# Part of a gate product moved into the recurrences of a four-layer stack, one addition moved to GpSimd, and new order lists

## The chip, the cores and the metric

The kernel runs on one core of a Trainium2 chip. Its time is in microseconds (us) of the device for one execution. TensorE is called PE (PEld is its loading of weights), VectorE DVE, ScalarE ACT, GpSimd POOL, and SP is the engine that issues all of this kernel's DMAs.

## The reference

The input x has 32 rows (batch) of 256 time steps with 256 features. Four layers are added to it one after the other; each has a condition of 256 features per row.

```python
x = x + L0(cond, x)   # GRU over time: z, r gates, hh = tanh(xh + r*h @ U + vh)
x = x + L1(cond, x)   # h = tanh(h * (1 - alpha) + sigmoid(h @ Wh.T + x_t @ Wz.T + b) * x_t)
x = x + L2(x, cond)   # gated cumulative sum
x = x + L3(x, cond)   # low-rank adapted MLP with gelu

# L2
f = sigmoid(x @ W_f.T + b_f);  i = sigmoid(x @ W_i.T + b_i)
gate_sum = f + i + EPS
candidate = x @ W_h.T + b_h
new_info = i / gate_sum * candidate
log_cumprod = cumsum(log(f / gate_sum + EPS), axis=1)
scaling = exp(log_cumprod[:, -1:] - padded[:, :-1])
hidden = cumsum(scaling * new_info) + exp(log_cumprod) * initial_hidden
```

L0 and L1 are recurrences: each of 256 steps needs the step before. The products of L2 (f, i and the candidate c) need only the finished x of their own time steps.

## The kernel before

**Two stages.** The first runs the two recurrences, step by step, layer 1 one step behind layer 0 (lines 726 to 804). The second runs the last layers, L2 and L3, over eight groups of four rows. The program fixes the order on every engine: each engine carries out its instructions in the order in which the code issues them.

**A step of the recurrences** issues on PE, in this order: U_rz (products of hT for the gates r and z), what falls due in the table `products`, w_1z (layer 1's product with its input, named w_l_Wz in the profile), U_h after r*h has been formed and transposed (rhT), w_1h, then W_rzh, the input products of the next step. `product` (line 601) cuts each into small products by quadrants of the array. Every fourth step a new bank of layer 0 is begun (line 633), every eighth one of layer 1 (at t % 8 == 2). On DVE a step has rh, rhT, keep (line 764), pieces of other work, the scan that forms h (line 672), hT, a transposition and the scan for layer 1. On POOL it has the residual of line 722 and the pairs of line 787.

**Tables of extra work.** `at(when, t, f, ...)` puts a piece of other work at step t in one of the tables products, sigmoids, sums, additions, moves, transfers; `due` issues it there. So the matrices of layer 3 are made (32 steps have such a product, line 507), and so are gates of L2: time is cut into NH = 8 stretches of CT = 32 steps, and once a stretch is finished, the gates f and i of its steps are computed for blocks of CB = 8 rows and halves e of the features. A unit (h, q, e) of `gate_unit` (line 103) has two tiles, f and i, each of two products over k; each product is 128x256. A free step takes one product; near the end five steps take two, which are then cut by quadrants. Then come the two sigmoids, the sum s = f + i (`add_up`), g = f + EPS*s (`guard`), and three stores into DRAM (`waiting`). This is done for the first NW_H = 6 of the 8 stretches.

**The last layers.** `STAGES` (line 967) names the pieces of work on a group: in (fetch the stored gates), lf, ls, lg (gates of the two late stretches, their sum and guard), c (`candidate`, the product with W_c over all eight stretches for two rows, 128x512), m (`weigh`, (c + b) * i on DVE), ln (logarithms on ACT), sum (the scan cc for the cumulative sum, DVE), w (`exponents`, one addition on DVE), exp (ACT), new and cum (DVE: times i, then a scan), h0 (DVE), x (`add_hidden`, an addition of 128x512 on POOL), mid, last and y (the two products and the end of layer 3). `HEAD` is the order of the first pieces, and `TURN` is the order for one turn; it is repeated for turns 2 to 9, where pieces of groups that do not exist are left out. A word such as `sum:1.0` is row 1, half 0 of the group. A turn works on several groups at once: stage 0 (lf to ln) on one group, sum and exp on the group before it, the rest on that or the one before.

`add_hidden` makes its POOL addition wait for the last DVE instruction that was issued ahead of it in the list (`on_vector`). On ACT, functions from another table need a table load (lines 846, 951, 1009).

Of the kernel before, what the change touches and what calls it, by code (L numbers as in the profile page):

```python
# [10 lines left out]
AF = mybir.ActivationFunctionType  # L11
ALU = mybir.AluOpType
# [4 lines left out]
B = 32  # L17
T = 256
# [11 lines left out]
CB = 8  # L30
NH = T // CT
NW_H = 6
EPS = 1e-8


# [4 lines left out]
def kernel(ctx: ExitStack, tc: tile.TileContext, a, out: bass.AP):  # L40
# [26 lines left out]
    def vec(name, c):  # L67
        i = VECS.index(name)
        return vecs[:, i, c : c + 1]
# [21 lines left out]
    def gate_product(ps, w, e, k, rows, h0, h1):  # L91

        nc.tensor.matmul(  # L93
            ps[:, 0 : (h1 - h0) * (rows.stop - rows.start) * CT].rearrange(
                "p (h b t) -> p h b t", h=h1 - h0, t=CT
            ),
            w[:, k, e * P : (e + 1) * P],
            X2[:, k, rows, h0 * CT : h1 * CT].rearrange("p b (h t) -> p h b t", t=CT),
            start=(k == 0),
            stop=(k == NC - 1),  # L100
        )

    def gate_unit(h, q, e, banks):

        t = {}

        def multiply(name, w, k, by_quadrants):
            rows = slice(q * CB, (q + 1) * CB)
            if not by_quadrants:
                gate_product(banks[name], w, e, k, rows, h, h + 1)  # L110
                return

            for j in range(Q):
                js = slice(j * SQ, (j + 1) * SQ)
                nc.tensor.matmul(
                    banks[name][js].rearrange("p (b t) -> p b t", t=CT),
                    w[:, k, e * P + js.start : e * P + js.stop],
                    X2[:, k, rows, h * CT : (h + 1) * CT],
                    start=(k == 0),
                    stop=(k == NC - 1),  # L120
                    skip_group_check=True,
                    tile_position=(0, j * SQ),
                )

        def unit_tile(name):
            t[name] = gu.tile([P, CB * CT], FP, name=f"gate_{name}", tag=f"gate_{name}")
            return t[name]

        def sigmoid(name):
            nc.scalar.activation(  # L130
                unit_tile(name), banks[name], AF.Sigmoid, bias=vec("b_" + name, e)
            )

        def add_up():
            nc.vector.tensor_add(unit_tile("s"), t["f"], t["i"])

        def guard():
            nc.vector.scalar_tensor_tensor(  # L138
                unit_tile("g"), t["s"], EPS, t["f"], ALU.mult, ALU.add
            )  # L140

        def store(name):
            nc.sync.dma_start(out=waiting[q][:, "gsi".index(name), e, h], in_=t[name])

        return multiply, sigmoid, add_up, guard, store

    parts_f = {}

# [19 lines left out]
    gi = ctx.enter_context(tc.tile_pool(name="gates_in", bufs=1))  # L168
    gated = {}

    def fetch_chunk(g, i, e, hs=slice(0, NW_H)):
        name = "gsi"[i]
        if e == hs.start == 0:
            pool, bufs = (gp, 2) if i == 2 and g % 3 else (gi, 1)
            gated[name, g] = pool.tile(
                [P, NC, NH, GB * CT], FP, name=f"in_{name}", tag=f"in_{name}", bufs=bufs
            )
        q, half = divmod(g, CB // GB)
        cols = slice(half * GB * CT, (half + 1) * GB * CT)
        nc.sync.dma_start(out=gated[name, g][:, e, hs], in_=waiting[q][:, i, e, hs, cols])  # L180

    def fetch(g, i):
        for e in range(NC):
# [16 lines left out]
    with ExitStack() as rec:  # L200
# [43 lines left out]
        def at(when, t, f, *args):  # L244
            when.setdefault(t, []).append((f, args))
# [307 lines left out]

        free = [t for t in range(CT + 3, T) if t not in products]
        twice = range(T - 14, T - 4, 2)
        free = sorted(free + list(twice))
        stored = {}
        for h in range(NW_H):  # L560
            for q in range(B // CB):
                for e in range(NC):
                    while free[0] < (h + 1) * CT + 3:
                        free.pop(0)
                    multiply, sigmoid, add_up, guard, store = gate_unit(
                        h, q, e, {"f": pg[:, 0], "i": pg[:, 1]}
                    )
                    for name, w in (("f", w_f), ("i", w_i)):
                        ts, free[:NC] = free[:NC], []
                        for k, t in enumerate(ts):  # L570
                            by_quadrants = any(t in twice for t in ts)
                            at(products, t, multiply, name, w, k, by_quadrants)
                        at(sigmoids, t, sigmoid, name)
                    at(sums, t + 1, add_up)
                    at(sums, t + 2, guard)
                    for n, name in enumerate("isg"):
                        stored[q] = t + 2 + n // 2 + (n == 2)
                        at(transfers, stored[q], store, name)
# [19 lines left out]
        def due(when, t):  # L598
            return [f(*args) for f, args in when.get(t, ())]
# [85 lines left out]
        def by_chunk(x):  # L685
            return x.rearrange("p (c b) -> p c b", b=B)
# [22 lines left out]
        with tc.manual_schedule():  # L709
# [16 lines left out]
            for t in range(T + 1):  # L726
# [15 lines left out]
                    finish_1()  # L742
                    late = None
                due(moves, t)
                due(products, t)
# [105 lines left out]
        )  # L851

    def late(g, name, e):
        return gated[name, g][:, e, LATE].rearrange("p h n -> p (h n)")

    def late_sum(g, e):
        return nc.vector.tensor_add(late(g, "s", e), parts_f[g, e], late(g, "i", e))
# [3 lines left out]
            late(g, "g", e), late(g, "s", e), EPS, parts_f.pop((g, e)), ALU.mult, ALU.add  # L861
        )

    def candidate(g, u):
        r, e = divmod(u, NC)
        b0 = g * GB + r * 2
        ps = pp.tile([P, 512], FP, name="ps_c", tag="ps_c")
        pcs[g, u] = ps.rearrange("p (h n) -> p h n", h=NH)
        for k in range(NC):
            gate_product(ps, w_n, e, k, slice(b0, b0 + 2), 0, NH)  # L870

    def weigh(g, u):
        r, e = divmod(u, NC)
        m = gated["i", g][:, e, :, r * 2 * CT : (r + 1) * 2 * CT]
        return nc.vector.scalar_tensor_tensor(
            m, pcs.pop((g, u)), vec("b_c", e), m, ALU.add, ALU.mult
        )

    def logs(g, q):
# [77 lines left out]
    def finish(g, b):  # L957
# [15 lines left out]
    }  # L973

    TURN = """
        lf:0 new:2 new:3 cum:2 sum:0.0 mid:1 in:2 mid:0 sum:1.0 cum:3 h0:2.0 lf:1 sum:0.1
        sum:3.1 last:1 sum:1.1 sum:3.0 w:1 exp:1 h0:3.1 h0:2.1 w:0 ls:0 h0:3.0 ls:1 c:0
        sum:2.0 w:3 lg:0 lg:1 x:2 m:0 y:1 x:3 exp:0 last:0 c:1 m:1 exp:3 c:3 y:0 mid:2 mid:3
        new:1 sum:2.1 new:0 w:2 cum:0 cum:1 c:2 h0:0.1 h0:0.0 exp:2 ln:1 h0:1.1 h0:1.0 ln:0
        last:2 x:1 m:3 last:3 y:2 in:1 x:0 m:2 in:0 y:3  # L980
    """

    HEAD = """
        in:2@2 lf:0@0 ls:0@0 lf:1@0 lg:0@0 c:2@0 c:1@0 ls:1@0 lg:1@0 ln:1@0 m:2@0 m:1@0
        sum:2.1@0 sum:2.0@0 c:0@0 ln:0@0 m:0@0 w:2@0 sum:3.1@0 sum:0.1@0 in:2@1 in:1@1
        sum:3.0@0 sum:0.0@0 sum:1.1@0 w:0@0 lf:0@1 lf:1@1 c:3@0 sum:1.0@0 ls:1@1 c:3@1 m:3@0
        exp:0@0 in:0@1 w:1@0 m:3@1 new:0@0 exp:1@0 lg:1@1 ls:0@1 new:1@0 w:3@0 exp:2@0
        cum:1@0 c:1@1 cum:0@0 h0:1.0@0 h0:0.0@0 exp:3@0 h0:1.1@0 lg:0@1 ln:1@1 x:1@0 ln:0@1
        c:2@1 m:1@1 c:0@1 h0:0.1@0 in:1@2 x:0@0 m:2@1 m:0@1 in:0@2
    """  # L990

    with tc.manual_schedule():
# [82 lines left out]
```

## Time and profile before

Three runs took 951.61 us at the median (950.96 to 952.18). The profiled execution has a span of 950.9 us.

| engine | busy, us | share of the span | instructions |
|---|---|---|---|
| PE | 919.3 | 97% | 22822 |
| DVE | 788.3 | 83% | 3409 |
| ACT | 573.3 | 60% | 2652 |
| POOL | 236.0 | 25% | 594 |

Some groups of the profile (line, engine, output from inputs, shape, count, busy us, mean ns of one):

| group | count | busy | mean |
|---|---|---|---|
| L93 PE ps_c from X, w_W_c, 128x512 | 128 | 61.5 | 613 |
| L93 PE pg from X, w_W_f, 128x256 | 176 | 61.5 | 431 |
| L938 PE ps_l from X, wt, 128x256 | 256 | 60.7 | 392 |
| L135 DVE gate_s from gate_f, gate_i, 128x256 | 48 | 22.2 | 462 |
| L875 DVE in_i from ps_c, vecs, in_i, 128x512 | 32 | 23.9 | 746 |
| L903 DVE w from cc, s, 128x512 | 32 | 21.7 | 678 |
| L960 DVE y from ps_l, X, 128x512 | 32 | 22.0 | 689 |
| L931 POOL X from X, w, 128x512 | 32 | 41.0 | 1291 |
| L722 POOL X from pairs, h1T, 128x64 | 256 | 102.7 | 401 |
| L467 POOL wn from wn, b, 128x128 | 16 | 7.2 | 450 |

How to read it: a product in fp32 shows as two records on PE. Busy time of a group counts overlapping instructions once; PE's ends are modelled, so for PE the distance from start to start tells more than the length. The recurrences run from 14 to about 736 us of the span, the last layers from there to the end.

### The profile page before, as it was taken

To read this page: it belongs to the slowest core of one execution; us is meant where nothing else is said; L and a number is where in the kernel's file an instruction comes from. 1 tells how busy PE (TensorE), PEld (TensorE's weight loads), DVE (VectorE), ACT (ScalarE), POOL (GpSimd) and SP (SyncE) were. 2 spreads that over 40 slices of the span, in tenths; PEclk is the share of its full clock that TensorE was granted. 3 is DMA by queue.
4 is the path that set the end of the run, shared out by engine and by line. 5 is a ranking of instruction groups with operands and counts; after the bars stand their busy time and mean duration, and the time that the engine had idled before them with its cause. 6 is when DMAs were issued, how large, how long until landed. Compare 5 with 4: busy or idle time off the path is not lost.

```text
span 950.9 us, 55227 instructions
## 1 busy us (share of the span) xinstructions
PE 919.3 (97%) x22822; PEld 630.0 (66%) x22822; DVE 788.3 (83%) x3409; ACT 573.3 (60%) x2652; POOL 236.0 (25%) x594
## 2 busy tenths in 40 slices
PE   7999999999999999999999999999999799999978
PEld 4666666666666666666666666666676467777756
DVE  5777788888888888888888888888877899999995
ACT  3455555555555555555555555555555878889973
POOL 1233322222222222222222222222222012222222
PEclk9999999999999999999999999999999999999989
DMA  8345212222222222222222222341232457777643
GB/s 259 114 118 156 80 52 87 71 73 91 70 88 78 86 76 66 92 71 87 72 72 92 66 92 66 121 131 61 83 115 74 132 166 231 230 219 223 190 156 124
DMA packets 109726, 107.72 MB, mean 113 GB/s; under 512 B 9857, under 2 KB 96673, under 8 KB 109474
## 3 DMA queue, kind: packets, MB, share of 16 engines
q1 hardware_dynamic: 109474, 104.19, 35.2%
q8 instruction: 179, 2.93, 1.4%
q14 instruction: 73, 0.60, 0.2%
HBM read 59.06 MB, written 45.09 MB: 110 GB/s over the span
## 4 chain that ended last, share of the span: by engine, by line
PE 81%; DVE 11%; ACT 3%; issue 2%; DMA 1%; SPq 0%; POOL 0%; DVEq 0%; POOLq 0%; ACTq 0%
PE p L606 46%; PE ps_l L938 11%; PE pg L93 10%; PE ps_c L93 5%; DVE h L672 5%; PE p L633 3%; PE ps_g L93 2%; PE pw L510 2%; ACT other L690 2%; DVE hT L682 1%; ACT r L690 1%; DVE cc L897 1%; DMA w_W_rzh<-in_W_rzh_dram 1%; DVE rh L760 1%; DVE gate_g L138 1%
## 5 line engine op out<-in xcount | busy, mean ns | idle before, releaser
L606 PE MATMUL p<-w_W_rzh,xT 128*32 128x192 f32 x4096 | 213.8, 326 | 0.7 <-DMA w_W_rzh<-in_W_rzh_dram 0.7
L690 ACT ACTIVATE other<-p 128x32 f32<-128x32 f32 x512 | 74.3, 200 | 171.6 <-PE p L606 171.6
L672 DVE TENSOR_TENSOR_SCAN h<-other,keep 128x64 f32<-128x64 f32 x512 | 121.3, 279 | 66.3 <-ACT other L690 62.9
L606 PE MATMUL p<-w_U_rz,hT 128*32 128x128 f32 x4080 | 166.1, 279 | 6.4 <-issue 0.3
L787 POOL TENSOR_TENSOR pairs<-xT,hT 128x64 f32<-128x64 f32 x256 | 82.3, 322 | 327.1 <-DVE other L803 301.9
L690 ACT ACTIVATE r<-p 128x32 f32<-128x32 f32 x510 | 72.8, 195 | 149.9 <-PE p L606 149.9
L722 POOL TENSOR_TENSOR X<-pairs,h1T 128x64 f32<-128x64 f32 x256 | 102.7, 401 | 214.7 <-DVE rhT L682 211.1
L606 PEld LDWEIGHTS p<-w_U_rz,hT 128*32 128x32 f32 x4080 | 97.0, 108 | 85.8 <-DVE hT L682 83.7
L672 DVE TENSOR_TENSOR_SCAN pre<-other,pairs 128x128 f32<-128x128 f32 x256 | 123.4, 482 | 33.9 <-ACT pairs L794 0.2
L606 PEld LDWEIGHTS p<-w_W_rzh,xT 128*32 128x32 f32 x4096 | 124.4, 110 | 22.9 <-DMA w_W_rzh<-in_W_rzh_dram 1.4
L606 PEld LDWEIGHTS p<-w_l_Wz,pairs 128*32 128x32 f32 x4096 | 78.2, 110 | 84.7 <-issue 69.3
L794 ACT ACTIVATE pairs<-h1T,leak 128x32 f32<-128x32 f32 x510 | 133.6, 314 | 0.4
L606 PE MATMUL p<-w_l_Wz,pairs 128*32 128x64 f32 x4096 | 119.2, 225 | 3.5 <-ACT keep L740 0.9
L606 PE MATMUL p<-w_U_h,rhT 128*32 128x64 f32 x4080 | 106.2, 221 | 0.0
L606 PE MATMUL p<-w_l_Wh,h1T 128*32 128x64 f32 x4080 | 104.1, 219 | 0.0
L760 DVE TENSOR_TENSOR rh<-r,h 128x32 f32<-128x32 f32 x510 | 75.0, 189 | 32.2 <-ACT r L690 6.2
L682 DVE STREAM_TRANSPOSE hT<-h 128x32 f32<-128x32 f32 x512 | 84.2, 198 | 0.0
L931 POOL TENSOR_TENSOR X<-X,w 128x512 f32<-128x512 f32 x32 | 41.0, 1291 | 162.3 <-DVE in_g L860 99.5
L682 DVE STREAM_TRANSPOSE rhT<-rh 128x32 f32<-128x32 f32 x510 | 80.0, 195 | 0.0
L606 PEld LDWEIGHTS p<-w_l_Wh,h1T 128*32 128x32 f32 x4080 | 76.2, 110 | 0.1
L606 PEld LDWEIGHTS p<-w_U_h,rhT 128*32 128x32 f32 x4080 | 69.6, 108 | 5.0
L719 ACT ACTIVATE h1T<-pre 128x64 f32<-128x64 f32 x256 | 69.7, 272 | 1.1 <-DVE pre L672 1.1
(110 smaller groups left out, 1472.7 us busy)
## 6 DMA issues: line engine op xcount, KB each, us to landing
adapted<-wm SPq DMA_DIRECT2D x128, 128.0 KB
wt<-adapted SPq DMA_DIRECT2D x28, 512.0 KB
w<-in_W_dram SPq DMA_DIRECT2D x32, 256.0 KB
out_dram<-y SPq DMA_DIRECT2D x32, 256.0 KB
xT<-in_xT_dram SPq DMA_DIRECT2D x60, 128.0 KB
gates<-gate_i SPq DMA_DIRECT2D x48, 128.0 KB
gates<-gate_s SPq DMA_DIRECT2D x48, 128.0 KB
gates<-gate_g SPq DMA_DIRECT2D x48, 128.0 KB
```

Of the source, the lines that this page charges most:

```text
L93: nc.tensor.matmul(ps[:, 0 : (h1 - h0) * (rows.stop - rows.start) * CT].rearrange("p (h b t) -> p h b t", h=h1 - h0, t=CT), w[:, k, e * P ...
L606: last = nc.tensor.matmul(ps[j * B : (j + 1) * B, cols], hT[:, k, :], w[:, k, j, :], start=False, stop=False, skip_group_check=True, tile_ ...
L672: nc.vector.tensor_tensor_scan(*(x[:, ns].rearrange("p n u -> p (n u)") for x in (done, other, pairs)), 0.0, ALU.mult, ALU.add,)
L682: nc.vector.transpose(dst[:, c], src[:, bass.ts(c, B)])
L690: nc.scalar.activation(dst[:, bass.ts(c, B)], src[:, bass.ts(c, B)], function)
L719: nc.scalar.activation(flat(h1T), pre, AF.Tanh)
L722: return nc.gpsimd.tensor_add(X2[:, :, :, s], by_chunk(pairs1.pop(s)[:, :, 0]), h1s.pop(s))
L760: rh_done = nc.vector.tensor_mul(rh[:, cs], r[:, cs], h[:, cs])
L787: nc.gpsimd.tensor_add(by_chunk(pairs1[t][:, :, 0]), x_of(t), hT)
L794: nc.scalar.activation(by_chunk(pairs1[s][:, :, 1])[:, c], h1T[:, c], AF.Copy, scale=leak[:, c : c + 1],)
L931: after(nc.gpsimd.tensor_add(x, x, ws[g][:, b]), on_vector)
L938: nc.tensor.matmul(ps[:, e, :], matrices[row][:, m, k, e * P : (e + 1) * P], src[:, k, :], start=(k == 0), stop=(k == NC - 1),)
```

## The change

The candidate's products of the first five stretches (NC_H = 5) and their weighing move into the recurrences. A unit there has now three tiles, f, i and c, in two PSUM banks used in turn; `weigh_unit` writes (c + b) * i over the tile i, which is then stored. Products go into the free steps one by one or, in steps called `doubled`, two at a time and cut by quadrants; in a doubled step layer 1's product w_1z is issued behind U_h. The sum s = f + i of a unit is made by GpSimd. In the last layers `candidate` and `weigh` do the three late stretches for all four rows at once (128x384), `exponents` is made by GpSimd, and `HEAD` and `TURN` are new lists.

```diff
+NC_H = 5
...
-    def gate_unit(h, q, e, banks):
+    def gate_unit(h, q, e):
...
         def add_up():
-            nc.vector.tensor_add(unit_tile("s"), t["f"], t["i"])
+            nc.gpsimd.tensor_add(unit_tile("s"), t["f"], t["i"])
...
+        def weigh_unit(bank):
+            nc.vector.scalar_tensor_tensor(
+                t["i"], bank, vec("b_c", e), t["i"], ALU.add, ALU.mult
+            )
...
+        begins = {t for t in range(T) if t % 4 in (0, 3)}
+        free = [t for t in range(CT + 3, T - 1) if t not in products]
+        wanted = [
+            (h, q, e, name) for h in range(NW_H) for q in range(B // CB) for e in range(NC)
+            for name in ("f", "i", "c")[: 3 if h < NC_H else 2]
+        ]
...
+        for n, (h, q, e, name) in enumerate(wanted):
...
+            bank, w = banks[n % 2], {"f": w_f, "i": w_i, "c": w_n}[name]
+            while free[0] < max((h + 1) * CT + 3, last_read[n % 2]):
+                free.pop(0)
+            short = NC * (len(wanted) - n) - len(free)
+            now = free.pop(0)
+            if short > 0 and (now not in begins or short > sum(t not in begins for t in free)):
+                doubled.add(now)
+            for k in range(NC):
+                if k and now not in doubled:
+                    now = free.pop(0)
+                at(products, now, multiply, bank, w, k, now in doubled)
+            if name == "c":
+                at(sums, now + 1, weigh_unit, bank)
...
+        for (h, q, e), t in ends.items():
+            _, _, add_up, guard, _, store = units[h, q, e]
+            at(sums, t + 1, add_up)
+            t += 2
+            while t in busy:
+                t += 1
+            busy.add(t)
+            at(sums, t, guard)
...
-                    done = product(p_1[s], cols_1(s), by_chunk(pairs1[s][:, :, 0]), w_1z)
-                    if run0:
-
-                        after(done, z_done)
+                    if t in doubled:
+                        after(multiplied[-1], z_done)
+                    else:
+                        done = product(p_1[s], cols_1(s), by_chunk(pairs1[s][:, :, 0]), w_1z)
+                        if run0:
+
+                            after(done, z_done)
...
                     product(p_0[t], cols_0(t, 2, 2), rhT, w_uh)
+                    if t in doubled:
+                        product(p_1[s], cols_1(s), by_chunk(pairs1[s][:, :, 0]), w_1z)
...
-    def candidate(g, u):
+    def candidate(g, e):
         ps = pp.tile([P, 512], FP, name="ps_c", tag="ps_c")
...
+            gate_product(ps, w_n, e, k, slice(g * GB, (g + 1) * GB), NC_H, NH)
...
     def exponents(g, b):
-        return nc.vector.tensor_add(ws[g][:, b], ccs[g][:, b, :, 0:T], ss[g][:, b])
+        nc.gpsimd.tensor_add(ws[g][:, b], ccs[g][:, b, :, 0:T], ss[g][:, b])
...
     TURN = """
-        lf:0 new:2 new:3 cum:2 sum:0.0 mid:1 in:2 mid:0 sum:1.0 cum:3 h0:2.0 lf:1 sum:0.1
-        sum:3.1 last:1 sum:1.1 sum:3.0 w:1 exp:1 h0:3.1 h0:2.1 w:0 ls:0 h0:3.0 ls:1 c:0
-        sum:2.0 w:3 lg:0 lg:1 x:2 m:0 y:1 x:3 exp:0 last:0 c:1 m:1 exp:3 c:3 y:0 mid:2 mid:3
-        new:1 sum:2.1 new:0 w:2 cum:0 cum:1 c:2 h0:0.1 h0:0.0 exp:2 ln:1 h0:1.1 h0:1.0 ln:0
-        last:2 x:1 m:3 last:3 y:2 in:1 x:0 m:2 in:0 y:3
+        lf:0 lf:1 sum:1.1 sum:0.0 sum:1.0 new:2 new:3 cum:2 sum:0.1 w:1 in:2 sum:3.0 h0:2.0 ls:1
+        sum:3.1 lg:1 cum:3 sum:2.0 ls:0 mid:0 h0:2.1 mid:1 c:0 last:0 w:0 w:3 x:2 h0:3.0 exp:1
+        new:1 h0:3.1 x:3 last:1 y:0 exp:3 lg:0 exp:0 sum:2.1 y:1 new:0 mid:2 mid:3 cum:1 w:2
+        cum:0 h0:0.1 h0:0.0 x:0 h0:1.0 ln:0 c:1 h0:1.1 m:1 exp:2 last:2 m:0 ln:1 x:1 y:2 last:3
+        y:3 in:1 in:0
     """
```

HEAD is rewritten in the same way, with the same kinds of pieces; it has now four c and four m in place of eight each. `in` on the gate tiles goes through a new function `gate_tile(name, g)`, which makes the tile on first use.

More of the change, by code (lines that the diff above doesn't have):

```diff
@@ L101, in gate_product, with multiply @@
         )
-    def gate_unit(h, q, e, banks):
+    def gate_unit(h, q, e):
         t = {}
-        def multiply(name, w, k, by_quadrants):
-            rows = slice(q * CB, (q + 1) * CB)
+        rows = slice(q * CB, (q + 1) * CB)
+        def multiply(bank, w, k, by_quadrants):
             if not by_quadrants:
-                gate_product(banks[name], w, e, k, rows, h, h + 1)
-                return
+                return gate_product(bank, w, e, k, rows, h, h + 1)
             for j in range(Q):
                 js = slice(j * SQ, (j + 1) * SQ)
-                nc.tensor.matmul(
-                    banks[name][js].rearrange("p (b t) -> p b t", t=CT),
+                done = nc.tensor.matmul(
+                    bank[js].rearrange("p (b t) -> p b t", t=CT),
                     w[:, k, e * P + js.start : e * P + js.stop],
@@ L123, in multiply @@
                 )
+            return done
         def unit_tile(name):
@@ L127, in unit_tile, with sigmoid @@
             return t[name]
[L129 to L132, printed above, removed]
+        def sigmoid(name, bank):
+            nc.scalar.activation(unit_tile(name), bank, AF.Sigmoid, bias=vec("b_" + name, e))
         def add_up():
-            nc.vector.tensor_add(unit_tile("s"), t["f"], t["i"])
+            nc.gpsimd.tensor_add(unit_tile("s"), t["f"], t["i"])
         def guard():
@@ L140, in guard @@
             )
+        def weigh_unit(bank):
+            nc.vector.scalar_tensor_tensor(
+                t["i"], bank, vec("b_c", e), t["i"], ALU.add, ALU.mult
+            )
         def store(name):
             nc.sync.dma_start(out=waiting[q][:, "gsi".index(name), e, h], in_=t[name])
-        return multiply, sigmoid, add_up, guard, store
+        return multiply, sigmoid, add_up, guard, weigh_unit, store
     parts_f = {}
@@ L169, with gate_tile @@
     gated = {}
[L171 to L174, printed above, removed]
+    def gate_tile(name, g):
+        if (name, g) not in gated:
+            pool, bufs = (gp, 2) if name == "i" and g % 3 else (gi, 1)
             gated[name, g] = pool.tile(
@@ L177, in fetch_chunk @@
             )
+        return gated[name, g]
+    def fetch_chunk(g, i, e, hs=slice(0, NW_H)):
+        name = "gsi"[i]
         q, half = divmod(g, CB // GB)
         cols = slice(half * GB * CT, (half + 1) * GB * CT)
-        nc.sync.dma_start(out=gated[name, g][:, e, hs], in_=waiting[q][:, i, e, hs, cols])
+        nc.sync.dma_start(out=gate_tile(name, g)[:, e, hs], in_=waiting[q][:, i, e, hs, cols])
     def fetch(g, i):
@@ L551 @@
             at(transfers, 26 + 2 * i, load_gate_weights, w, name)
[L556 to L578, printed above, removed]
@@ new lines @@
+        banks = pg[:, 0], pg[:, 1]
+        begins = {t for t in range(T) if t % 4 in (0, 3)}
[4 more added lines that the diff above has]
+        ]
+        stored, units, ends, last_read = {}, {}, {}, [0, 0]
+        doubled, busy = set(), set()
+        for n, (h, q, e, name) in enumerate(wanted):
+            if name == "f":
+                units[h, q, e] = gate_unit(h, q, e)
+            multiply, sigmoid, add_up, guard, weigh_unit, store = units[h, q, e]
+            bank, w = banks[n % 2], {"f": w_f, "i": w_i, "c": w_n}[name]
[11 more added lines that the diff above has]
+                at(sums, now + 1, weigh_unit, bank)
+                busy.add(now + 1)
+                last_read[n % 2] = now + 2
+                at(transfers, now + 2, store, "i")
+                stored[q] = max(stored.get(q, 0), now + 2)
+            else:
+                at(sigmoids, now, sigmoid, name, bank)
+                last_read[n % 2] = now + 1
+            if name == "i":
+                ends[h, q, e] = now
@@ L579 @@
+        for (h, q, e), t in ends.items():
[6 more added lines that the diff above has]
+            at(sums, t, guard)
+            if h >= NC_H:
+                at(transfers, t, store, "i")
+            at(transfers, t, store, "s")
+            at(transfers, t + 1, store, "g")
+            stored[q] = max(stored.get(q, 0), t + 1)
         first_late = [
@@ L744 @@
                 due(moves, t)
-                due(products, t)
+                multiplied = due(products, t)
                 if t == T:
@@ L750 @@
                         begin_1(0, U1_0)
-                    done = product(p_1[s], cols_1(s), by_chunk(pairs1[s][:, :, 0]), w_1z)
-                    if run0:
-                        after(done, z_done)
+                    if t in doubled:
+                        after(multiplied[-1], z_done)
+                    else:
+                        done = product(p_1[s], cols_1(s), by_chunk(pairs1[s][:, :, 0]), w_1z)
+                        if run0:
+                            after(done, z_done)
                 rh_done = kept_done = None
@@ L853, in late @@
     def late(g, name, e):
-        return gated[name, g][:, e, LATE].rearrange("p h n -> p (h n)")
+        return gate_tile(name, g)[:, e, LATE].rearrange("p h n -> p (h n)")
     def late_sum(g, e):
@@ L862, in late_guard, with weigh @@
         )
-    def candidate(g, u):
-        r, e = divmod(u, NC)
-        b0 = g * GB + r * 2
+    def candidate(g, e):
         ps = pp.tile([P, 512], FP, name="ps_c", tag="ps_c")
-        pcs[g, u] = ps.rearrange("p (h n) -> p h n", h=NH)
+        pcs[g, e] = ps[:, 0 : (NH - NC_H) * GB * CT]
         for k in range(NC):
[L870 to L874, printed above, removed]
+            gate_product(ps, w_n, e, k, slice(g * GB, (g + 1) * GB), NC_H, NH)
+    def weigh(g, e):
+        m = gated["i", g][:, e, NC_H:NH].rearrange("p h n -> p (h n)")
         return nc.vector.scalar_tensor_tensor(
-            m, pcs.pop((g, u)), vec("b_c", e), m, ALU.add, ALU.mult
+            m, pcs.pop((g, e)), vec("b_c", e), m, ALU.add, ALU.mult
         )
@@ L975 @@
     TURN = """
-        lf:0 new:2 new:3 cum:2 sum:0.0 mid:1 in:2 mid:0 sum:1.0 cum:3 h0:2.0 lf:1 sum:0.1
-        sum:3.1 last:1 sum:1.1 sum:3.0 w:1 exp:1 h0:3.1 h0:2.1 w:0 ls:0 h0:3.0 ls:1 c:0
-        sum:2.0 w:3 lg:0 lg:1 x:2 m:0 y:1 x:3 exp:0 last:0 c:1 m:1 exp:3 c:3 y:0 mid:2 mid:3
-        new:1 sum:2.1 new:0 w:2 cum:0 cum:1 c:2 h0:0.1 h0:0.0 exp:2 ln:1 h0:1.1 h0:1.0 ln:0
-        last:2 x:1 m:3 last:3 y:2 in:1 x:0 m:2 in:0 y:3
+        lf:0 lf:1 sum:1.1 sum:0.0 sum:1.0 new:2 new:3 cum:2 sum:0.1 w:1 in:2 sum:3.0 h0:2.0 ls:1
[3 more added lines that the diff above has]
+        y:3 in:1 in:0
     """
     HEAD = """
[L984 to L989, printed above, removed]
+        in:2@1 lf:1@0 ls:1@0 lf:0@0 c:0@0 lg:1@0 ls:0@0 lg:0@0 ln:0@0 sum:0.0@0 sum:0.1@0 ln:1@0
+        sum:1.0@0 lf:1@1 sum:2.0@0 c:1@0 in:2@2 sum:2.1@0 sum:1.1@0 sum:3.0@0 m:1@0 ls:1@1 w:1@0
+        w:0@0 sum:3.1@0 lf:0@1 in:1@1 m:0@0 w:2@0 exp:1@0 exp:0@0 new:1@0 ls:0@1 c:0@1 cum:1@0
+        in:0@1 exp:2@0 c:1@1 new:0@0 lg:0@1 lg:1@1 w:3@0 h0:1.1@0 ln:1@1 cum:0@0 h0:1.0@0
+        h0:0.0@0 h0:0.1@0 x:1@0 ln:0@1 x:0@0 exp:3@0 m:0@1 in:0@2 m:1@1 in:1@2
     """
```

## The prediction

> **What bounds the kernel now.** I read first the table of busy time by stretches, then the chain of waits in order of time, then timelines of single steps. The columns of the first are the stretch, its length, then busy time and instructions of PE, PEld, DVE, ACT and POOL, the granted clock, the DMA share and GB/s. One row is from the recurrences (from 14 to 736 us), one from the last layers (736 to 951):
>
> ```profile
> 300.00:400.00 100.00, 99.24 (x3064) 66.23 (x3057) 84.04 (x436) 55.49 (x336) 26.05 (x72) 1.00 0.25 78
> 840.00:860.00 20.00, 20.00 (x78) 14.27 (x77) 19.78 (x35) 17.41 (x27) 3.70 (x3) 1.00 0.78 236
> ```
>
> In the last layers PE is full, DVE nearly so (19.78 of 20), POOL almost idle. The chain there is PE alone from 759.6 to 909.6 us; one turn of it (start, length, what):
>
> ```profile
> 836.83 1.73 PE ps_g L93 x8
> 838.56 3.45 PE ps_l L938 x16
> ...
> 848.91 3.65 PE ps_c L93 x8
> ...
> 861.18 1.73 PE ps_g L93 x8
> ```
>
> A turn over a group of four rows is 861.18 - 836.83 = 24.35 us. DVE is busy some 97% of that (mean of the five rows from 780 to 880), 23.7 us. So a change must relieve both: DVE would set 23.7 at once.
>
> In the recurrences a step is 2.80 us between the sigmoids of line 740. It is a loop of short works (hT, U_rz, r, rh, rhT, U_h, tanh, h, hT), and PE fills its two gaps. Here is a step of before with two gate products in it, by start and length:
>
> ```profile
> 693.76 0.61 PE L115 MATMUL pg<-X,w_W_i 128*32 128x256 f32 x8
> 694.20 0.61 PE L115 MATMUL pg<-X,w_W_f 128*32 128x256 f32 x8
> 694.63 0.41 PE L606 MATMUL p<-w_l_Wz,pairs 128*32 128x64 f32 x16
> 694.85 0.41 PE L606 MATMUL p<-w_U_h,rhT 128*32 128x64 f32 x16
> 695.08 0.41 PE L606 MATMUL p<-w_l_Wh,h1T 128*32 128x64 f32 x16
> 695.30 0.83 PE L606 MATMUL p<-w_W_rzh,xT 128*32 128x192 f32 x16
> 695.95 0.40 PE L633 MATMUL p<-parts,eye 128*32 128x512 bf16 x4
> 696.19 0.64 PE L606 MATMUL p<-w_U_rz,hT 128*32 128x128 f32 x16
> ```
>
> From start to start, a product by quadrants takes 0.44 us, the three small products 0.22 each, W_rzh 0.65, the begin of eight steps of layer 1 about 0.22. Such a step takes 2.885, 0.09 more than the others, because U_h starts 1.55 after U_rz (693.30), not 1.45.
>
> The third reading is what the whole forecast hangs on: GpSimd's adds and VectorE's instructions with two SBUF inputs do not run side by side.
>
> ```profile
> 758.81 0.76 DVE L875 SCALAR_TENSOR_TENSOR in_i<-ps_c,vecs,in_i 128x512 f32<-128x512 f32 x1
> 759.48 1.13 DVE L924 SCALAR_TENSOR_TENSOR w<-cc,condT,w 128x256 f32<-128x256 f32 x1
> ...
> 759.05 1.27 POOL L931 TENSOR_TENSOR X<-X,w 128x512 f32<-128x512 f32 x1 [21.50 <-DVE in_g L860]
> ```
>
> L875 reads PSUM and one SBUF tile, and takes its usual 0.75 beside the add. L924 reads two SBUF tiles, usually takes 0.47, here 1.13: it ends at 760.61, 0.29 after the add. The scan of L897 (usually 0.68) took 1.75 at 923.44 under another such add, which itself took 1.71, not 1.28, after meeting L915. In all of the steady turns of before, the X adds lie beside L875 and L960 (both read PSUM), so this costs almost nothing there.
>
> The Trainium skill (SBUF — State Buffer, "SBUF: two separate sides") says the same as a rule, and it speaks against this change: a VectorE instruction with two SBUF inputs and a GpSimd instruction that reads SBUF exclude each other for a whole instruction. By a whole 1.29 per add my 1.1 below would be some 0.2 larger; the rows decide.
>
> **The change, part by part: the recurrences.**
>
> *More products.* 48 units of f and i, and 40 of c, are 136 tiles, 272 products of 128x256. Steps from 35 to 254 without an adapter's matrices are 220 - 32 = 188, so 84 steps hold two products by quadrants (before: 5). In them w_l_Wz moves behind U_h. First gap: U_rz 0.46, then 2 x 0.44 = 1.34 us, under the 1.45 at which rhT comes: no loss, and 0.09 x 5 = 0.45 us gained back. The last of these products now waits for the sigmoid z, which ends at 694.42 in the step above, while that product starts near 694.6: nothing. Second gap: U_h, w_l_Wz, w_l_Wh at 0.22 and W_rzh 0.65 end at 1.45 + 1.31 = 2.76, under 2.80: hidden, by 0.04. Where layer 1 begins eight steps (t mod 8 = 2; 27 of the 84) 0.22 comes on top: 2.98, +0.18 each, 4.9 us. Where layer 0 begins (t mod 4 = 0 or 3; 9 of them), 0.16: +0.12, 1.1 us. The other 48 cost 0 to 0.09. Bounds: 0 (PE catches up over the next step) and 84 x 0.18 = 15.
>
> *add_up on GpSimd, 48 times.* This shape isn't in the trace; between 128x128 (L467, 0.450) and 128x512 (L931, 1.29) it comes to 0.725. It follows the residual of line 722 in POOL's queue. The timeline shows such a place with the smaller add:
>
> ```profile
> 37.50 0.40 POOL L722 TENSOR_TENSOR X<-pairs,h1T 128x64 f32<-128x64 f32 x1 [0.82 <-DVE rhT L682]
> 37.85 0.45 POOL L467 TENSOR_TENSOR wn<-wn,b 128x128 f32<-128x128 f32 x1
> 38.28 0.47 DVE L672 TENSOR_TENSOR_SCAN h<-other,keep 128x64 f32<-128x64 f32 x2 [0.58 <-ACT other L690]
> ```
>
> The add of 0.45 is over when the scan for h, which has two SBUF inputs and lies on the loop, really reads. An add of 0.725 ends at 37.85 + 0.725 = 38.575; the scan would read from about 38.38 (0.1 after its start, as L924's delay implies). So h, hT and the next U_rz are late by about 0.17: 48 x 0.17 = 8.2 us. Bounds: 0 (the scan wins) and 0.25, 12 us. In 6 of these steps the layer 1 begin already costs 0.18, and the two overlap: -1.0. The next in POOL's queue, L787, is not due before 39.14. DVE's 48 additions of 0.46 go away, but they hid before (steps with one take the same 2.80).
>
> *weigh_unit, 40 times.* From PSUM, 128x256: L875 is 0.07 over an SBUF add of its size (0.746 to 0.678), so 0.42 + 0.06 = 0.48. 29 of them share a step with a piece of L522, and at 326.69 the row of L135 (0.41) beside a piece ends just as the scan for h starts: 29 x 0.06 = 1.7 us, 0 to 3. The stores of in_i wait for it on SP's queue, where only other stores and prefetches stand: nothing.
>
> Loop: 4.9 + 1.1 + 8.2 - 1.0 + 1.7 - 0.45 = 14.5 us, from 3 to 25.
>
> **The last layers.** *PE* loses ps_c: 16 records of 0.43 per turn go, 8 of 384 columns (0.32) come: 24.35 - 7.1 + 2.6 = 19.9. *ACT* (17.5 of 20 in the same five rows, 21.3 per turn) loses one of six table loads (1.28): 20.0. *DVE* loses four exponents (L903, 0.60 from start to start) and four weighings at 0.67 for two of about 0.55: 23.7 - 2.4 - 1.6 = 19.7. If nothing else came, a turn could be some 20 us.
>
> *POOL* has eight adds of 1.24 per turn in place of four, 9.9 us. Of DVE's 19.7 only L875 and L960 (1.1 + 2.4 = 3.5) may run beside them; 16.2 may not. Even with all 3.5 used, both together need about 16.2 + 9.9 - 0.8 (DVE's start of 0.1 hidden eight times) = 25.3, over the 24.35 of before. The new list, by where each add becomes free: w:1 after sum:1.0 (then new, new, cum), w:0 after sum:0.1 (sum, h0), w:3 after sum:3.1 (lg, cum), x:2 after h0:2.1 (h0, new), x:0 after h0:0.0 (h0): five before instructions with two SBUF inputs, each holding DVE some 1.1 (1.24 less its start and the hidden start of the one that waits). x:3 before y:0 and w:2 before y:1 have 0.6 hidden: 0.55 each. x:1 before m:1, m:0, y:2, y:3: nothing. A turn: 19.7 + 5 x 1.1 + 2 x 0.55 = 26.3, +2.0. Six full turns +12; the turn without new gates +1; the head 0 (it loses four exponents and half its weighings, about 5 us of DVE, and takes four adds of 1.1 in their place; -2 to +2). Together +13. Bounds: from -25 (no exclusion: 20.8 per turn, and 4 us from the head and the end) to +25 (all eight exposed, 28.5 per turn).
>
> **Sum.** 950.9 + 14.5 + 13 = 978.4 for the profiled execution, whose span stands 0.7 below the median of 951.6: 979 us.
>
> **The rivals.** *A, faster:* POOL's adds find DVE waiting, or DVE always wins, and turns are set by ACT and PE at 20.8 us. For: PE, ACT and DVE all fall, and the X adds are free now. Against: they are free beside PSUM readers only. -25 with half of the loop's cost, +8: 934. Chance 0.16. *B, slower by less:* the scan for h wins, PE catches up, the turn sits at its 25.2: 951.6 + 5 + 5 = 962. For: the loop's margins are of hundredths. Chance 0.20. *C, no change,* gain in one stage against loss in the other: 951, 0.03. *D, far slower:* every step with two products loses 0.18, every add is exposed: 951.6 + 24 + 25 = 1000. For: the second gap has only 0.04 left. Chance 0.07.
>
> **Numbers.** The forecast has 0.54, from 966 to 991; with B the range is 954 to 992. A measurement of this kernel tells about 0.2%, 2 us, from no change. Faster 0.17 (A and a little of C), same 0.03, slower 0.80.
>
> **What would show it.** The scan for h should last or start about 0.17 later in steps with add_up on POOL; steps with two products at t mod 8 = 2 should be near 2.98 and the others 2.80. In the last layers the turn (from one ps_g to the next) should be near 26, PE with gaps, and L915, L920, L897 or L924 lengthened by up to 1.1 beside an exponents add. A turn near 20 with those lines at their usual lengths would make the forecast wrong.

## The result and the profile after

The changed kernel takes 981.38 us at the median (980.2 to 982.83); the kernel before, on the same chip, 951.89. The ratio is 1.0307 (95% interval 1.0289 to 1.0325): slower. The forecast was 979 us. The profiled execution has a span of 979.2 us, 28.3 over that of before. The loop is counted here from the first sigmoid z to the last.

| stretch, us | before | changed | difference | forecast |
|---|---|---|---|---|
| up to the first sigmoid z | 13.8 | 14.5 | +0.7 | 0 |
| recurrences, first to last z | 717.6 | 737.5 | +19.9 | +14.5 |
| from the last z to the end | 219.5 | 227.2 | +7.7 | +13 |

Busy time by stretches (stretch, its length, then PE, PEld, DVE, ACT, POOL, clock, DMA share, GB/s) of the changed kernel:

```profile
300.00:400.00 100.00, 99.34 (x3123) 69.78 (x3120) 82.09 (x424) 54.55 (x323) 29.46 (x76) 1.00 0.24 77
840.00:860.00 20.00, 16.63 (x66) 13.32 (x65) 19.90 (x28) 15.27 (x23) 9.20 (x7) 0.91 0.66 187
860.00:880.00 20.00, 15.76 (x61) 12.78 (x60) 20.00 (x26) 14.82 (x22) 9.35 (x8) 0.83 0.86 254
```

In the last layers PE has gaps now, ACT too, and DVE is full. Its instructions are fewer than before in such a stretch (28 and 26, not 35 and 34), though: they got longer. The granted clock of PE is lower as well, 0.91 and 0.83 in these two rows where both had 1.00 before. A slower PE is a rival that the prediction did not name; it does not set the turn, since DVE is busy for 19.90 and 20.00 of 20 us. From 760 to 800 us, where the clock was 0.83 and 0.86 and DVE not full at first, its share is not separated. The timelines of DVE and of POOL in one turn (start, length):

```profile
862.34 2.16 DVE L949 TENSOR_TENSOR w<-in_i,w 128x512 f32<-128x512 f32 x2
...
866.72 1.41 DVE L958 SCALAR_TENSOR_TENSOR w<-cc,condT,w 128x256 f32<-128x256 f32 x1
...
869.31 2.11 DVE L954 TENSOR_TENSOR_SCAN w<-anew,w 128x512 f32<-128x512 f32 x1
...
877.86 1.39 DVE L949 TENSOR_TENSOR w<-in_i,w 128x512 f32<-128x512 f32 x1
```

```profile
862.59 1.36 POOL L937 TENSOR_TENSOR w<-cc,s 128x512 f32<-128x512 f32 x1 [1.84 <-DVE cc L931]
...
866.29 1.56 POOL L937 TENSOR_TENSOR w<-cc,s 128x512 f32<-128x512 f32 x1 [2.35 <-DVE cc L931]
...
869.21 1.12 POOL L937 TENSOR_TENSOR w<-cc,s 128x512 f32<-128x512 f32 x1 [1.36 <-DVE cc L931]
...
877.43 1.26 POOL L937 TENSOR_TENSOR w<-cc,s 128x512 f32<-128x512 f32 x1 [0.96 <-DVE cc L931]
```

Each exponents add meets a DVE instruction with two SBUF inputs, and that one takes 1.58 for 0.68 (the second of the two L949), 1.41 for 0.47, 2.11 for 1.21, 1.39 for 0.68. It ends 0.55, 0.28, 1.09 and 0.56 us after the add, which is its own usual length less 0.1 to 0.2: it does its work only when the add is over. That is 3.5 us per turn for the four. The X adds, which have lost their cover in the new list, cost 2.9 in the same way. Together 6.4, so that 19.7 us of own work (the prediction's estimate) become a turn of 26.09 us (mean of five, from the last y of one group to that of the next).

In the loop, a step with one product and add_up on POOL, first POOL's timeline, then DVE's:

```profile
373.29 0.41 POOL L754 TENSOR_TENSOR X<-pairs,h1T 128x64 f32<-128x64 f32 x1 [0.83 <-DVE rhT L714]
373.65 0.73 POOL L134 TENSOR_TENSOR gate_s<-gate_f,gate_i 128x256 f32<-128x256 f32 x1
```

```profile
374.09 0.62 DVE L704 TENSOR_TENSOR_SCAN h<-other,keep 128x64 f32<-128x64 f32 x2 [0.58 <-ACT other L722]
374.63 0.32 DVE L714 STREAM_TRANSPOSE hT<-h 128x32 f32<-128x32 f32 x2
```

The add takes 0.73, the estimate was 0.725. The scan for h begins under it at its usual time and has to wait: its two halves take 0.62, where they take 0.47 in a step without a sum. Single steps (one product or none) with a sum take 2.957 us at the median, against 2.80.

The steps with two products, called doubled, are the surprise. At the median they take 2.92 us, 3.04 where layer 0 begins a bank, and 3.09 where layer 1 does. PE's timeline in one of the last kind:

```profile
179.12 1.15 PE L115 MATMUL pg<-X,w_W_c 128*32 128x256 f32 x16
180.01 0.43 PE L638 MATMUL p<-w_U_h,rhT 128*32 128x64 f32 x15
180.24 0.23 PE L638 MATMUL p<-w_l_Wz,pairs 128*32 128x64 f32 x3
180.28 0.22 PE L638 MATMUL p<-w_U_h,rhT 128*32 128x64 f32 x1
180.29 0.38 PE L638 MATMUL p<-w_l_Wz,pairs 128*32 128x64 f32 x12
...
181.33 0.48 PE L665 MATMUL p<-parts,eye 128*32 128x512 bf16 x4
181.55 0.70 PE L638 MATMUL p<-w_U_rz,hT 128*32 128x128 f32 x16
```

The gate products reach to 180.27 (by ends that are modelled), past the start of U_h at 180.01, and the sixteenth record of U_h starts only at 180.28, behind records of w_l_Wz that were issued after it. So on PE the order of issue does not hold between quadrants, and U_h is over late because one quadrant of the array comes free late. At the end the begin of layer 1 stands right before U_rz.

### The profile page after: what moved, and what is told of

Same layout as the page of the kernel before. It is cut to its first block, busy times and chain, and to the rows that moved or that the text cites. A ratio compares the mean times of both kernels' runs of the same rounds, so it can differ in the third digit from the quotient of the medians.

```text
span 979.2 us, 57372 instructions
## 1 busy us (share of the span) xinstructions
PE 922.3 (94%) x23830; PEld 664.8 (68%) x23830; DVE 804.5 (82%) x3353; ACT 572.4 (58%) x2646; POOL 317.0 (32%) x674
## 4 chain that ended last, share of the span: by engine, by line
PE 77%; DVE 13%; ACT 4%; issue 2%; POOL 2%; DMA 1%; SPq 0%; DVEq 0%; ACTq 0%; POOLq 0%
PE p L638 48%; PE pg L115 9%; PE pg L94 7%; PE ps_l L972 6%; PE p L665 3%; DVE w L954 3%; DVE cc L931 2%; DVE h L704 2%; PE pw L517 2%; DVE w L949 2%; POOL X L965 1%; DVE w L958 1%; ACT other L722 1%; DMA w_W_rzh<-in_W_rzh_dram 1%; DVE y L994 1%
## 5 line engine op out<-in xcount | busy, mean ns | idle before, releaser
L638 PE MATMUL p<-w_W_rzh,xT 128*32 128x192 f32 x4096 | 226.2, 326 | 0.7 <-DMA w_W_rzh<-in_W_rzh_dram 0.5
L754 POOL TENSOR_TENSOR X<-pairs,h1T 128x64 f32<-128x64 f32 x256 | 102.6, 401 | 221.0 <-DVE rhT L714 213.8
L638 PEld LDWEIGHTS p<-w_W_rzh,xT 128*32 128x32 f32 x4096 | 134.9, 110 | 23.2 <-issue 2.1
L638 PE MATMUL p<-w_l_Wz,pairs 128*32 128x64 f32 x4096 | 128.2, 223 | 2.6 <-ACT keep L772 0.6
L638 PEld LDWEIGHTS p<-w_l_Wz,pairs 128*32 128x32 f32 x4096 | 89.7, 110 | 58.1 <-issue 45.3
L638 PE MATMUL p<-w_U_h,rhT 128*32 128x64 f32 x4080 | 118.3, 221 | 0.0
L638 PE MATMUL p<-w_l_Wh,h1T 128*32 128x64 f32 x4080 | 115.7, 219 | 0.1
L972 PE MATMUL ps_l<-X,wt 128*128 128x256 f32 x256 | 73.1, 448 | 33.8 <-POOL X L965 31.2
L638 PEld LDWEIGHTS p<-w_U_h,rhT 128*32 128x32 f32 x4080 | 82.7, 108 | 14.6
L972 PEld LDWEIGHTS ps_l<-X,wt 128*128 128x128 f32 x256 | 57.6, 229 | 48.3 <-POOL X L965 34.8
L638 PEld LDWEIGHTS p<-w_l_Wh,h1T 128*32 128x32 f32 x4080 | 87.2, 110 | 0.5 <-issue 0.5
```

Source lines behind the costliest of these rows:

```text
L638: last = nc.tensor.matmul(ps[j * B : (j + 1) * B, cols], hT[:, k, :], w[:, k, j, :], start=False, stop=False, skip_group_check=True, tile_ ...
L754: return nc.gpsimd.tensor_add(X2[:, :, :, s], by_chunk(pairs1.pop(s)[:, :, 0]), h1s.pop(s))
L972: nc.tensor.matmul(ps[:, e, :], matrices[row][:, m, k, e * P : (e + 1) * P], src[:, k, :], start=(k == 0), stop=(k == NC - 1),)
```

## The experiments

Chips differ a little; each run is compared with the kernel before on its own chip. Summary first (turn and loop from the profiles, one of each run). The loop of the changed kernel, in the same code, reads 737.5, 740.5 and 740.4 in the first three runs that have it, so a difference of some 3 us between two loops tells nothing.

| run | median us | before there | ratio (95%) | loop | after it | turn |
|---|---|---|---|---|---|---|
| changed | 981.38 | 951.89 | 1.0307 (1.0289 to 1.0325) | 737.5 | 227.2 | 26.09 |
| exponents on DVE | 975.94 | 954.97 | 1.0220 (1.0199 to 1.0240) | 740.5 | 219.3 | 25.04 |
| sums on DVE | 980.19 | 954.97 | 1.0260 (1.0243 to 1.0277) | 735.5 | 228.2 | |
| memsets for exponents | 956.19 | 954.97 | single run | 740.4 | 201.2 | 22.57 |
| later wait for z | 995.10 | 954.97 | 1.0417 (1.0382 to 1.0452) | 752.5 | 227.1 | |
| later wait for z, again | 987.98 | 953.29 | single run | 745.4 | 227.5 | |
| w_1z in the first gap | 975.59 | 955.25 | 1.0215 (1.0177 to 1.0252) | 729.6 | 227.3 | |
| before, exponents on POOL | 960.06 | 955.25 | 1.0053 (1.0033 to 1.0073) | 717.2 | 225.7 | 25.24 |
| before, sums on POOL | 961.46 | 953.29 | 1.0092 (1.0073 to 1.0112) | 725.1 | 219.9 | |
| moves and lists alone | 962.27 | 954.30 | 1.0080 (1.0060 to 1.0100) | 726.9 | 219.3 | 25.04 |
| two stretches, old lists | 950.77 | 955.25 | 0.9949 (0.9931 to 0.9968) | 722.0 | 213.8 | 23.60 |
| one stretch, old lists | 952.15 | 954.30 | 0.9974 (0.9963 to 0.9985) | 721.9 | 214.9 | 23.85 |

### Exponents back on DVE

```diff
     def exponents(g, b):
-        nc.gpsimd.tensor_add(ws[g][:, b], ccs[g][:, b, :, 0:T], ss[g][:, b])
+        return nc.vector.tensor_add(ws[g][:, b], ccs[g][:, b, :, 0:T], ss[g][:, b])
```

> The changed kernel with the exponents back on VectorE, all else as changed. Theory (GpSimd's adds and VectorE's instructions with two SBUF inputs exclude each other): VectorE gets 4 x 0.60 us back per turn and loses the four waits of 0.7 to 1.0 us each that the exponents caused; a turn goes from 26.1 to about 24.9 us, the time from 981 to 973 to 976. Rival (the new lists put the work in an order with long waits, or the moved products do it): VectorE only gets more work, a turn stays at 26 us or grows, 980 to 990.

The turn fell to 25.04 and the stretch behind the loop from 227.2 to 219.3, with 2.4 us more work per turn on DVE. The theory holds, the rival falls: with DVE as the full engine, more work on it cannot shorten a turn unless waits go.

### Memsets in place of the exponents

```diff
-        nc.gpsimd.tensor_add(ws[g][:, b], ccs[g][:, b, :, 0:T], ss[g][:, b])
+        for e in range(NC):
+            after(nc.gpsimd.memset(ws[g][:, b], 0.0), sums_of[g, b, e])
```

> The changed kernel with each exponents addition on GpSimd replaced by two memsets of the same tile, which wait for the same scans; the addition itself is left out. GpSimd is busy about as long (2 x 0.51 us for 1.29), but reads nothing from SBUF. Theory (it is the reading that excludes VectorE): the waits of L949, L954 and L958 beside the exponents go, VectorE needs 19.7 us of its own and some 2.8 us beside the X adds, a turn takes about 22.5 us, the time 958 to 964. Rival (GpSimd is late with the exponents, or the order of the lists): a turn stays at 25.5 us or more, 975 to 980.

In this run the exponents are left out and the tile is filled with zeros. The turn is 22.57 us (22.5 expected). The time is even lower than expected, because the head and the end shrink as well (201.2 us behind the loop). The timelines of DVE and POOL show instructions of the same lines beside GpSimd at their own length:

```profile
873.49 1.26 DVE L951 TENSOR_TENSOR w<-in_i,w 128x512 f32<-128x512 f32 x2
874.67 1.21 DVE L956 TENSOR_TENSOR_SCAN w<-anew,w 128x512 f32<-128x512 f32 x1
```

```profile
873.62 1.57 POOL L939 MEMSET w<- 128x512 f32 x3 [1.72 <-DVE cc L931]
```

Two L951 in 1.26 and L956 in 1.21 under three memsets: GpSimd at work is no hindrance, GpSimd reading SBUF is.

### The kernel before, with only the exponents on GpSimd

```diff
-        return nc.vector.tensor_add(ws[g][:, b], ccs[g][:, b, :, 0:T], ss[g][:, b])
+        nc.gpsimd.tensor_add(ws[g][:, b], ccs[g][:, b, :, 0:T], ss[g][:, b])
```

> The kernel before, with its own lists and no product moved, and only the exponents given to GpSimd. Theory (exclusion): VectorE's 23.7 us per turn lose 4 x 0.60 and get four waits of 0.7 to 1.1 us, while the X adds keep their cover: 24.1 to 25.7 us per turn in place of 24.35, PE is no longer full, the time is 0 to 9 us above that of before, most likely 5. Rival (an addition on the almost idle GpSimd is free, the loss of the change comes from its lists): PE's 24.35 us stay, the head and the end get shorter, 1 to 4 us below before.

4.8 us above before, the turn 25.24: the addition costs more than it saves also under the old lists and without any move. DVE's timeline there, then POOL's:

```profile
846.81 2.66 DVE L924 SCALAR_TENSOR_TENSOR w<-cc,condT,w 128x256 f32<-128x256 f32 x2
849.39 1.31 DVE L857 TENSOR_TENSOR in_s<-gate_f,in_i 128x256 f32<-128x256 f32 x1
```

```profile
846.48 3.94 POOL L903 TENSOR_TENSOR w<-cc,s 128x512 f32<-128x512 f32 x3 [7.03 <-DVE cc L897]
```

Three adds in a row let through two L924 and one L857 in some 4 us; alone these take 0.47, 0.47 and 0.42. This run settles the rival of the clock for the exponents, too: PE keeps 1.00 in the steady turns here, as in this stretch of its last layers (columns as above), and the turn is longer all the same.

```profile
840.00:860.00 20.00, 19.16 (x75) 13.66 (x74) 19.96 (x28) 16.55 (x25) 8.06 (x6) 1.00 0.83 257
```

### The sums f + i: back on DVE, and alone on GpSimd in the kernel before

```diff
         def add_up():
-            nc.gpsimd.tensor_add(unit_tile("s"), t["f"], t["i"])
+            nc.vector.tensor_add(unit_tile("s"), t["f"], t["i"])
```

> The changed kernel with the 48 sums f + i of the recurrences back on VectorE. Theory: the 22 single steps with a sum fall from 2.957 to 2.80 us, the 16 doubled ones by 0.05, those where layer 1 begins by nothing: 22 x 0.157 + 16 x 0.05 = 4.3 us less, 977. Rival (the steps with a sum are long for another reason, such as their products): no more than 1 us less.

Single steps with a sum fell from 2.957 to 2.82, doubled ones from 2.96 to 2.92, those with a begin not at all: 3.0 + 0.6 = 3.6 us. The ratio to before fell from 1.0307 to 1.0260, some 4.5 us: the theory's 4.3 holds, and the rival falls. (The two medians, 981.38 and 980.19, come from different chips.) It is not 48 x 0.16, because in 25 of the 48 steps two products cost nearly as much as the sum, and the two do not add.

The opposite edit, in the kernel before:

> The kernel before with only the 48 sums f + i of the recurrences given to GpSimd. Theory (the sum holds the scan for h back for as long as it reads): each step with a sum takes 2.957 us in place of 2.80, 48 x 0.157 = 7.5 us above before; the last layers stay. Rival (the sum hides in a single step, and was only seen beside other changes): within 1 us of before.

The steps with a sum take 2.955 us, the loop 7.5 us more than in the profile of before, and the time is 8.2 us above before on the same chip. In these steps the first half of the scan lasts 0.447 us at the median, in the others 0.292: the whole 0.155 is there. This is the term by itself.

### The steps with two products

```diff
-                    if t in doubled:
-                        after(multiplied[-1], z_done)
-                    else:
+                    if t not in doubled:
...
                     if t in doubled:
-                        product(p_1[s], cols_1(s), by_chunk(pairs1[s][:, :, 0]), w_1z)
+                        done = product(p_1[s], cols_1(s), by_chunk(pairs1[s][:, :, 0]), w_1z)
+                        after(done, z_done)
```

> The changed kernel where, in steps with two products, the early wait for the sigmoid z stands at the last of layer 1's products behind U_h, not at the last of the gate products. Theory (the last gate product waits for z, starts late and holds the last quadrant of U_h for 0.12 us): plain doubled steps fall from 2.92 to 2.80 us, those with a begin from 3.04 and 3.09 to 2.92 and 2.97; where a sum on GpSimd sets 2.957 only 0.02 is gained: some 7.5 us less in all, 974. Rival (the second gap is overfull with layer 1's product in it): within 2 us of 981.

Neither. Doubled steps fell only to 2.885, 3.00 and 3.05, so the early wait is worth 0.035 us, not 0.12. U_h starts 1.53 us after U_rz in a plain doubled step of this run, and 1.45 in a single one: the two products alone, without w_1z in the gap, make it late by 0.08. The kernel as a whole got slower, through irregular steps of 3.2 to 3.8 us.

> The kernel with the later wait for z once more, on another chip, to see whether its irregular steps of 3.2 to 3.7 us come from the kernel or from that run. From the kernel (another wait of PE takes the place of the one removed): again 30 or more steps over 3.15 us, some 10 us above the changed kernel. From the run: as many as the changed kernel has (4), doubled steps at 2.885, 3.00 and 3.05, and 976 to 980 us.

It took 987.98 us in a single run, with before at 953.29. From step 35 on there are 20 steps over 3.15 us there, 37 in the first profile, and 4 in the changed kernel. 17 of the 20 stand at the same steps as in the first profile (51, 82, 106, 214, 218, 220 and so on), so most of them belong to the kernel. In many of them PE stands idle, for up to 0.6 us (its weight loading for up to 0.8), where the profile shows nothing that it waits for:

```profile
250.63 0.39 PE L638 MATMUL p<-w_l_Wz,pairs 128*32 128x64 f32 x10
...
251.49 0.26 PE L638 MATMUL p<-w_l_Wz,pairs 128*32 128x64 f32 x3 [0.47 <-issue]
```

This pair is from the timeline of the first of the two profiles. The cause of these gaps stays open. The traces hold one sign: in the loops of the two profiles neither products nor weight loads run for over 0.25 us 24 times (never in the changed kernel, once in the kernel before), and 23 of these gaps end 1.06 to 1.68 us ahead of the next transfer on the DMA queue that the profile calls q8 instruction, whose transfers come some 4 us apart. So the supply of instructions is a suspect; no run tests it.

The other way round, w_1z back in the first gap:

```diff
-                    if t in doubled:
-                        after(multiplied[-1], z_done)
-                    else:
-                        done = product(p_1[s], cols_1(s), by_chunk(pairs1[s][:, :, 0]), w_1z)
...
+                    done = product(p_1[s], cols_1(s), by_chunk(pairs1[s][:, :, 0]), w_1z)
...
-                    if t in doubled:
-                        product(p_1[s], cols_1(s), by_chunk(pairs1[s][:, :, 0]), w_1z)
```

> The changed kernel with layer 1's product w_1z back in the first gap in steps with two products, and its early wait for z there too, as the kernel before has it. Theory (its place behind U_h makes the second gap overfull where a begin stands, and adds nothing but cost elsewhere): every doubled step takes about 2.89 us as the five of before, in place of 2.92, 3.04 and 3.09; with the sums on GpSimd in the way (2.957) some 8 us less than the changed kernel in the loop. Rival (84 steps with two products are too much for PE wherever w_1z stands): 2.95 to 3.1 us in each, no more than 2 us less.

All kinds of doubled steps take 2.887 us at the median (2.96 with a sum), the loop is 7.9 us shorter. So two products cost 0.09 wherever w_1z stands, and its new place costs 0.03, 0.15 or 0.20 on top; 0.035 of each is the early wait.

### All three undone, and a version that is faster

> The changed kernel with all three of its costs undone: exponents and sums back on VectorE, w_1z in the first gap. What is left is the move of five stretches and the new lists. Theory: the loop pays 79 x 0.09 = 7 us over before, the last layers take about the 219 us of before (a turn of 24.9, as measured with the exponents back on VectorE): 5 to 8 us above before. Rival (the costs found so far overlap, so that undoing all gains more than their sum): at or below before.

With the exponents and sums on DVE and w_1z in the first gap, what is left is 8.0 us above before: the loop pays 9.3, and the last layers give back 0.2. PE has been relieved of over 4 us per turn by the prediction's sum, but DVE needs 25.04, of which 2.9 are waits beside the X adds.

So fewer stretches, and the old lists, which keep the X adds beside weighings and y:

```diff
-NC_H = 5
+NC_H = 2
...
-        pcs[g, e] = ps[:, 0 : (NH - NC_H) * GB * CT]
+        pcs[g, u] = ps[:, 0 : (NH - NC_H) * 2 * CT].rearrange("p (h n) -> p h n", h=NH - NC_H)
         for k in range(NC):
-            gate_product(ps, w_n, e, k, slice(g * GB, (g + 1) * GB), NC_H, NH)
+            gate_product(ps, w_n, e, k, slice(b0, b0 + 2), NC_H, NH)
```

(with `TURN` and `HEAD` of before, the sums and exponents on DVE, and w_1z in the first gap)

> A version meant to be faster: the candidate's products and their weighing moved for two stretches only, w_1z in the first gap, all additions on VectorE as before, and the old lists, whose units of two rows now take six stretches (384 columns). Theory: 36 doubled steps in place of 5 cost 31 x 0.09 = 2.8 us; a turn needs 22.6 us of PE and 23.2 of VectorE in place of 24.35, some 5 to 6 us less over the last layers: 2 to 4 us below before. Rival (shorter weighings no longer cover the X adds, so VectorE waits beside them): a turn of 24.3 us or more and a time 2 to 4 us above before.

0.5% faster than before, the fastest version run: the turn is 23.60 us, the loop pays 4.4. The rival's wait is there in small:

```profile
852.14 0.61 DVE L907 SCALAR_TENSOR_TENSOR in_i<-ps_c,vecs,in_i 128x384 f32<-128x384 f32 x1
852.67 0.68 DVE L992 TENSOR_TENSOR y<-ps_l,X 128x512 f32<-128x512 f32 x1
853.26 1.04 DVE L947 TENSOR_TENSOR w<-in_i,w 128x512 f32<-128x512 f32 x1
```

These rows of DVE's timeline stand beside two X adds (851.25 to 853.76). L907 and L992 read PSUM and keep their length; L947 comes 0.5 us too early and takes 1.04, not 0.68.

> As the version with two stretches, but with one stretch moved. Theory: 20 doubled steps in place of 36 (16 x 0.09 = 1.4 us less), PE needs 23.5 us per turn and VectorE 23.4 with the X adds better covered, so a turn stays near the 23.66 us measured with two: 1 to 2 us below that version, some 5 to 6 us below before. Rival (PE and VectorE are then both nearly full and wait for each other): a turn near 24.2, 1 to 3 us below before only.

0.26% faster: by the medians a smaller gain than with two, though the two intervals overlap a little. The turn is 23.85 and not 23.66, and the loop's 1.4 us did not show (721.9 and 722.0, less than two profiles can tell).

## Why the prediction was right, and where it was wrong inside

- **The exclusion of GpSimd's adds and DVE's two-input instructions** was right, and it is shown: the adds taken away, replaced by work that does not read, or added alone changed the turn by what it says. The turn was forecast at 26.3 and is 26.09; the waits were 6.6 and are 6.4. With the exponents' adds replaced by memsets, a single run stands only 1.2 us above before, so these waits make up most of the loss.
- **"Six full turns +12"** was mis-sized. From the end of the first full turn to the end of the last there are five turns, 5 x 1.74 = 8.7 us. The head with its first turn got 1.3 shorter (56.8 to 55.5), and with the exponents back on DVE it is 1.6 shorter still, so it gained by the moved work in spite of the adds; the end is within 0.4 of before. Hence +7.7, not +13.
- **"First gap: ... no loss"** failed. Two products by quadrants cost 0.09 in every step, as in the five steps of before, though w_l_Wz is gone from the gap: U_h comes at 1.53 without it. So it was not w_l_Wz that made those five late. The sum of starts (1.34 under 1.45) left out that a quadrant is busy past the last start (by the modelled ends, to 1.51), and that U_h must have all four; this reason is read from the rows, and no run tests it apart.
- **"The last of these products now waits for the sigmoid z ... nothing"** failed by 0.035 us.
- **The second gap** was sized well. Over the plain doubled step of the run with the later wait (2.885), a begin of layer 1 costs 0.17 (forecast 0.18) and one of layer 0 0.12 (0.12). The 0.12 that each of the 84 steps costs beyond the forecast is the first gap's 0.085 with the wait's 0.035. In all, the 84 steps cost some 17.5 us over 2.797 each, sums in them included, where 6.0 was forecast.
- **The sums on GpSimd** were right by the step (0.16 for 0.17; the prediction's own figures, 38.575 - 38.38, give 0.195), but not in number: 25 of the 48 stand in doubled steps, which are late anyway. Singles cost 22 x 0.16 = 3.5 us, and the forecast let only 6 overlap: 7.2. Alone, in the kernel before, all 48 count: 7.5 us.
- **weigh_unit** cost 0.02 in a step, not 0.06.
- **PE's sum** has a slip: 16 records of 0.43 are 6.9 us, not 7.1. It changes nothing, since PE did not set the turn.
- The loop was forecast 5.4 us too low and the last layers 5.3 too high: the total of 979 owes its closeness to two errors that cancelled, which is luck. The direction and the turn are not.

## What to carry to other kernels

An idle engine is not a free one: before work goes from DVE to GpSimd, count which of DVE's instructions read two SBUF tiles, and treat those and GpSimd's reading instructions as one queue. Relieve all engines that are nearly full in a stage, or the next one sets it: here over 4 us of PE per turn bought nothing once DVE stood behind it. Delays that lie beside each other in one step of a loop are to be compared, not added (a sum and two products together take 2.96, alone 2.96 and 2.92); delays one after the other on an engine do add (0.085 for two products and 0.17 for the begin behind them). And the sum of the products' starts does not tell when a gap on PE is full: here it gave 1.34 of 1.45 us, and U_h came at 1.53.

## What was not expected of the hardware

- Gaps of up to 0.6 us on PE without any wait that the profile shows, mostly at the same steps in two runs and at a steady place between two transfers of the queue called instruction, after an edit that only moved one semaphore wait. The loop was 5 to 15 us longer with them (745.4 and 752.5, against 737.5 to 740.5 with the loop of the changed kernel).
- GpSimd's memsets of 128x512 (0.52 us each) run beside DVE's two-input instructions with no sign of each other.
- With three GpSimd adds in a queue, adds and DVE instructions take turns: 1.29, 1.45 and 1.27 us for the adds, and two L924 and one L857 let through, one after each add.
